# Routing two tiles further ahead, and the scatters of the gap in small lots

## The chip, the core and the metric

The kernel runs on one core of one Trainium2 chip. Its time is the device time of one execution in microseconds (us). The kernel before took 792.53 us as a median of three runs (790.85 to 795.97). A core has five engines that run their own instruction streams: TensorE (PE, whose weight loads are listed as PEld), VectorE (DVE), ScalarE (ACT), GpSimd (POOL) and SyncE (SP). They wait for one another through semaphores. POOL issues the indirect DMAs (rows sent to places that a list of numbers names), SP nearly all others.

## The reference

The input x has 4096 tokens of width 256. The reference computes, in float32:

```python
q = layernorm(x)
h = softmax((q@Wq+bq) (ctx@Wk+bk)^T per head)    # 16 heads, 77 keys
o = h @ (ctx@Wv+bv) @ Wo + bo
x = x + gamma * layernorm(q + o, eps=1e-3) + beta
f = layernorm(x)
weights, experts = top_k(softmax(f @ Wg), 4)     # 32 experts
y = sum over a token's 4 experts of weight * (silu(f@W1[e]) * (f@W3[e])) @ W2[e]
out = x + y + (silu(f@Ws1) * (f@Ws3)) @ Ws2      # the shared FFN
```

An expert takes at most 2048 (token, expert) pairs.

## The kernel before

**Stages.** Up to about 60 us the weights are prepared: Wk is folded with Wq, and Wv with Wo. Then comes the loop over 32 tiles of 128 tokens (t = 0 to 31; eight blocks of four tiles, `blk = t // 4`, `c = t % 4`), from 64 to about 394 us. Behind it stands a stretch, here called the gap, in which the shared FFN of three blocks is computed (y = block 6, block 0 and z = block 7, in this order) and the last two blocks are routed. It ends in the expert phase, which runs over tiles of 128 rows of one expert, about 1.63 us each, from about 474 to 705 us, with the shared FFN of the other blocks among them. The results are gathered and stored by 793.7.

**One tile of the loop.** `scores` makes the scores of 16 heads in three groups on PE (L430) and their maxima on DVE (L438). `soften` takes the exponentials on ACT (L446), head by head, with their sums. `invert` makes the reciprocals on DVE (L456), and `divide` multiplies on POOL (L461, three instructions of 0.97 us). One tile later `turn_p` transposes the probabilities on PE (L479), with copies on DVE (L484) and ACT (L484, L487, L488), `output` multiplies them with the folded values (L497), and `residual` adds the result and measures it (L505, L355, L356, DVE). So within tile t the order on DVE is: maxima of t, a copy for t-1, invert of t, other work, residual of t-1, and then the first maximum of t+1.

**Block work in the loop.** `scale_in`, `norm_in`, `turn_in` and `bias_in` prepare the next block's input. `keep` (L403, DVE) lays x + beta aside. `settle` (L523, L526, L355, L356, DVE) finishes the attention of one tile and measures it for the second layernorm; POOL makes the reciprocal deviations in `measure_out` and `measure_ffn`, and `norm_ffn` (ACT, with `shift`, L361, on DVE) normalises.

**Routing of a block** follows its settling, in this order: `turn_ffn` (PE transposes, ACT copies, L553, a store by SP), `gate` (L566, PE), `turn_gate` (L579, L581), `chances` (L589, L590), `powers` (ACT, L594), `choose` (top four, L603 to L612, DVE), `mark` (one-hot form of the choice, its sums and the running counts, L619, L626, L630, DVE), `count` (L638, PE), `place` (L654 to L664, DVE, three small operations on POOL). Then `send` (L674) scatters the 512 tokens' rows to the places of their experts in device memory, in 16 indirect DMAs of 128 rows: each takes POOL 0.96 us and 0.30 us of issue. `tables("a")` and `tables("z")` turn the counts into tables of the expert tiles' rows and experts; "a" covers the first 64 expert tiles, which read rows of blocks 0 to 5 only. `fetch` reads such a table into registers of SP and loads eight tiles' rows.

**What sets the order.** Nothing is planned: inside `with as_written()` every instruction of an engine is made to follow the one written before it. The one exception is a run of scatters: instructions within it have no order among themselves, so the scheduler may swap them. The routing of block `blk - 2` is written into block `blk`'s tiles: `turn_ffn` in c0; `gate`, `turn_gate`, `chances`, `powers` and `choose` in c1; `mark` in c2 ahead of `invert`; `count` and `place` in c3. Four scatters are sent per tile from t = 11. Three tiles of a block are settled one per tile behind `invert` in c0, c1 and c2, the first tile already in its own block's c3, and `keep` does two tiles in c2 and two in c3. After the loop 44 scatters are left: 12 of block 5, then 16 each of y and z. They are sent in groups of 3, 2, 7, 12 and 20.

Of the kernel before, what the change touches and what calls it, by code (L numbers as in the profile page):

```python
# [30 lines left out]
def kernel(  # L31
# [73 lines left out]
    iota_j = const.tile([P, NJ], F32, name="iota_j")  # L105
    nc.gpsimd.iota(iota_j, [[1, NJ]], base=0, channel_multiplier=0, allow_small_or_imprecise_dtypes=True)
# [260 lines left out]
    def means(name):  # L367
        return sm.tile([P, NC, 2], F32, tag="mv", name=f"mv_{name}", bufs=6)
# [300 lines left out]
    def send(blk, i0, i1):  # L669

        row, xn = rows[blk], xns[blk]
        for i in range(i0, i1):
            c = i // TOPK
            sct = nc.gpsimd.indirect_dma_start(  # L674
                out=xr,
                out_offset=bass.IndirectOffsetOnAxis(ap=row[:, i : i + 1], axis=0),
                in_=xn[:, c, :],
                in_offset=None,
            )


            tc.declare_no_dep(sct.ins, group="rows", reason="distinct rows")
            tc.add_to_no_dep_group("rows", sct.ins)
            scatters.append(sct.ins)
            if blk < BA:
                early.append(sct.ins)
            else:

                tc.declare_no_dep(sct.ins, group="firsts", reason="distinct rows")
                tc.add_to_no_dep_group("lates", sct.ins)  # L690

# [56 lines left out]
    measure_in(0)  # L748
    scale_in(0)
    norm_in(0)  # L750
    turn_in(0)
    bias_in(0)
    keep(0, 0, NC)
    xts[1] = load(1)
    with as_written():
        for t in range(NT):
            blk, c = t // NC, t % NC
            ffn, old = blk - 1, blk - 2
            ahead = blk + 1 < NB
            if c == 0 and blk + 2 < NB:  # L760
                xts[blk + 2] = load(blk + 2)
            if t == 0:

                nc.sync.dma_start(xr[NE * PLACES :, :], none)
                nc.sync.dma_start(
                    xr[: NE * PLACES, :].rearrange("(e q) r -> q e r", q=PLACES)[:P],
                    none.unsqueeze(1).to_broadcast([P, NE, ROW]),
                )
            if t == 18:
                nc.sync.dma_start(ws13[:, :, 0, :], Ws1.rearrange("(k p) f -> p k f", p=P))  # L770
                nc.sync.dma_start(ws13[:, :, 1, :], Ws3.rearrange("(k p) f -> p k f", p=P))
                nc.sync.dma_start(ws2, Ws2.rearrange("(k p) f -> p k f", p=P))
            if t in parts:
                load_experts(*parts[t])
            if c == 1 and ahead:
                scale_in(blk + 1)
            if c == 1 and ffn >= 0:
                measure_out(ffn, 2, 4)
            if c == 3 and ahead:
                bias_in(blk + 1)  # L780
            if c == 3:
                measure_out(blk, 0, 2)
            if c == 3 and ffn >= 0:
                measure_ffn(ffn)
            if c == 1 and old >= 0:
                gate(old)
            if c == 3 and old >= 0:
                count(old)
            sv = [scores(t, g) for g in range(2)]
            if c == 1 and old >= 0:  # L790
                turn_gate(old)
                chances(old)
            soften(t, 0, sv[0])
            if c == 1 and old >= 0:
                powers(old)
            soften(t, 1, sv[1])
            sv.append(scores(t, 2))
            if t >= 1:
                for i in range(3):
                    turn_p(t - 1, i)  # L800
            soften(t, 2, sv[2])
            if c == 0 and old >= 0:
                turn_ffn(old)
            if c == 2 and ahead:
                turn_in(blk + 1)
            if c == 0 and ahead:
                measure_in(blk + 1)
            if c == 1 and old >= 0:
                choose(old)
            if c == 2 and old >= 0:  # L810
                mark(old)
            if c == 3 and old >= 0:
                place(old)
            invert(t)
            divide(t)
            if c == 1 and ahead:
                norm_in(blk + 1)
            if c == 3 and ffn >= 0:
                norm_ffn(ffn)
            if c == 3:  # L820
                settle(blk, 0)
            elif ffn >= 0:
                settle(ffn, c + 1)
            if c >= 2 and ahead:
                keep(blk + 1, 2 * c - 4, 2 * c - 2)
            if t >= 11:
                b11, c11 = divmod(t - 11, NC)
                send(b11, c11 * TOPK, (c11 + 1) * TOPK)
            if t >= 1:
                residual(t - 1, output(t - 1))  # L830

        sxs[0] = late.tile([P, NC, D], F32, tag="qb", name="sx_0", bufs=3)
        sxs[0] = sxs[0].rearrange("p c d -> p (c d)").rearrange("p (k t) -> p k t", k=KC)
        nc.sync.dma_start(sxs[0], xnd[0])
        z, y = NB - 1, NB - 2
        assert BA == y
        msum_a = sm.tile([P, NE], F32, tag="msum_a", name="msum_a", bufs=1)
        nc.vector.tensor_copy(msum_a, cums[BA][:, 0, :])  # L840
        left = [(y - 1, i) for i in range(NK)]

        def sends(n):
            for blk, i in left[:n]:
                send(blk, i, i + 1)
            del left[:n]

        del left[:4]
        measure_out(z, 2, 3)
        settle(z, 1)  # L850
        sends(3)
        turn_ffn(y)
        for i in range(3):
            turn_p(NT - 1, i)
        settle(z, 2)
        residual(NT - 1, output(NT - 1))
        measure_out(z, 3, 4)
        gate(y)
        turn_gate(y)
        chances(y)  # L860
        powers(y)
        settle(z, 3)
        sends(2)
        measure_ffn(z)
    att_stack.close()

    hs_stack = ExitStack()
    hs = hs_stack.enter_context(tc.tile_pool(name="hs", bufs=1))
    tb = hs_stack.enter_context(tc.tile_pool(name="tb", bufs=1))


    tabs = {}
    e_col = tb.tile([NE, P], F32, name="e_col")
    k_a = tb.tile([NE, 1], F32, name="k_a")

    def tables(which, pairs, n):


        def small(name, dt=F32):
            return tb.tile([NE, 1], dt, tag=f"{name}_{which}", name=f"{name}_{which}")  # L880

        def wide(name, p=NE, dt=F32):
            return tb.tile([p, n], dt, tag=f"{name}_{which}" if p != NE else name, name=f"{name}_{which}")
# [12 lines left out]
        if first:  # L896
            nc.vector.tensor_scalar(e_col, ones[:NE, :], iota_p[:NE, :], None, ALU.mult)
        else:
# [20 lines left out]
        oj, t1, t2 = wide("oj"), wide("t1"), wide("t2")  # L919
        nc.vector.tensor_scalar(oj, iota_j[:NE, :n], start, None, ALU.is_ge)  # L920
        nc.vector.tensor_scalar(t1, iota_j[:NE, :n], end, None, ALU.is_ge)
# [3 lines left out]
        nc.vector.tensor_scalar(t2, iota_j[:NE, :n], base, float(P), ALU.subtract, ALU.mult)  # L925
# [5 lines left out]
        nc.vector.scalar_tensor_tensor(t2, t2, first_e, oj, ALU.add, ALU.mult)  # L931
        yield
# [3 lines left out]
        nc.tensor.matmul(p_e[:, :n], e_col, oj, start=True, stop=True)  # L936
# [11 lines left out]
        if not first:  # L948
# [3 lines left out]
            n_i = tb.tile([1, 1], I32, name="n_i")  # L952
            nc.vector.tensor_scalar(n_i, p_n[0:1, 0:1], float(RG - 1 + NA - NM_), 0.0, ALU.add, ALU.max)
            n_more = tb.tile([1, 1], I32, name="n_more")
# [3 lines left out]

    with as_written():
        for part in range(5):  # L960
            load_experts(*parts[NT + 1 + part])
        ta = tables("a", msum_a, NA)
        choose(y)
        shared_in(y, 0, AF.Tanh)
        norm_ffn(z)
        mark(y)
        sends(7)
        shared_mid(y, 0)
        next(ta)
        shared_in(y, 1, AF.Tanh)  # L970
        turn_ffn(z)
        count(y)
        gate(z)
        next(ta)
        place(y)
        assert not left
        left += [(y, i) for i in range(NK)]
        turn_gate(z)
        chances(z)
        powers(z)  # L980
        next(ta)
        shared_mid(y, 1)
        shared_in(0, 0, AF.Silu)
        choose(z)
        shared_out(y)
        next(ta)
        mark(z)
        shared_mid(0, 0)
        shared_in(0, 1, AF.Silu)
        count(z)  # L990
        msum_z = sm.tile([P, NE], F32, tag="msum_z", name="msum_z", bufs=1)
        nc.vector.tensor_copy(msum_z, cums[NB][:, 0, :])
        tz = tables("z", msum_z, NJ - NA)
        sends(12)
        place(z)
        left += [(z, i) for i in range(NK)]
        shared_mid(0, 1)
        shared_in(z, 0, AF.Silu)
# [321 lines left out]
```

## Time and profile before

| | |
|---|---|
| median of three runs | 792.53 us |
| the profiled execution | 795.5 us, of which its span 793.7 us |
| PE busy | 726.8 us, 92% of the span |
| DVE busy | 526.8 us, 66% |
| POOL busy | 403.3 us, 51% |
| ACT busy | 334.3 us, 42% |
| scatters, L674 | 128, 127.8 us busy on POOL |

Busy time is the time in which an instruction of the engine ran. In the rows that follow, a group's line, engine and operation come first, then output and input with their shapes and a count; `idle` or a bracket gives the time that the engine stood still just before, and the instruction that ended this. "remote" and "another core or an unknown queue" mean that the release could not be put down to an instruction. PEclk is the share of full clock that TensorE was granted.

### The profile page before, as it was taken

How to read it: one execution, taken by the hardware profiler on the slowest of the kernel's cores; microseconds unless marked ns; L12 is line 12 of the kernel's file. 1: busy time of each engine (PE TensorE's matmuls, PEld its weight loads, DVE VectorE, ACT ScalarE, POOL GpSimd, SP SyncE). 2: the span in 40 equal slices, each digit the busy share in tenths (PEclk: the TensorE clock that was granted, in tenths of full speed). 3: DMA queues.
4: the chain of work that ended last, by engine and by line, in shares of the span. 5: the costliest groups of instructions: out<-in, count | busy, mean ns of one | idle time of the engine just before them, and what ended most of it. 6: DMA issues, size and time to landing. Idle time of an engine off the chain costs nothing.

```text
span 793.7 us, 12911 instructions
## 1 busy us (share of the span) xinstructions
PE 726.8 (92%) x3508; PEld 540.2 (68%) x3508; DVE 526.8 (66%) x1455; ACT 334.3 (42%) x1586; POOL 403.3 (51%) x488
## 2 busy tenths in 40 slices
PE   6999999999999999999975569999999999999883
PEld 4775777677777777776743347888888878776452
DVE  1874565787778777776753336666667666564797
ACT  0647666766667776766621002222222222221100
POOL 2003333346878777786887354555555555534000
PEclk9999999999999999999999688999999999999997
DMA  8930000403226131514183523465655544522997
GB/s 270 331 107 1 1 0 2 124 10 114 79 72 213 58 130 57 155 51 142 57 243 107 159 94 110 143 209 178 210 159 170 166 158 143 175 89 74 404 396 282
DMA packets 78866, 111.96 MB, mean 141 GB/s; under 512 B 9995, under 2 KB 63679, under 8 KB 78783
## 3 DMA queue, kind: packets, MB, share of 16 engines
q1 hardware_dynamic: 59663, 66.66, 27.0%
q0 software_dynamic: 13056, 36.72, 12.8%
q10 hardware_dynamic: 6064, 7.64, 2.8%
q8 instruction: 31, 0.51, 0.3%
q14 instruction: 52, 0.43, 0.2%
HBM read 62.36 MB, written 48.64 MB: 140 GB/s over the span
## 4 chain that ended last, share of the span: by engine, by line
PE 66%; DVE 12%; ACT 6%; DMA 4%; another core or an unknown queue 4%; POOL 3%; issue 3%; SPq 0%; DVEq 0%; ACTq 0%; POOLq 0%
PE peh L1097 15%; PE po L497 14%; PE sc L430 13%; PE py L1118 7%; ACT p L446 5%; PE pgT L1089 4%; PE pp L479 2%; DVE gy L1213 2%; PE phT L1111 2%; PE ph L704 2%; DMA gy<-ys 2%; DVE y L1214 1%; POOL xr L674 1%; PE pvo L262 1%
## 5 line engine op out<-in xcount | busy, mean ns | idle before, releaser
L1123 POOL DMA_INDIRECT ys<-y,place x144 | 138.5, 962 | 120.7 <-DVE y L1122 81.0
L446 ACT ACTIVATE p<-sc,mx 128x77 f32<-128x77 f32 x512 | 159.5, 352 | 93.1 <-DVE mx L438 93.1
L1097 PE MATMUL peh<-we,gT 128*128 x576 | 151.9, 387 | 7.6 <-DVE gT L1091 7.1
L497 PE MATMUL po<-we,pT 128*128 128x256 f32 (+1 forms) x640 | 147.4, 384 | 4.6 <-DVE pT L484 3.3
L674 POOL DMA_INDIRECT xr<-xn,row x128 | 127.8, 999 | 46.5 <-issue 35.1
L461 POOL TENSOR_TENSOR p<-p,su 128x385 f32<-128x385 f32 (+1 forms) x96 | 91.1, 974 | 97.4 <-DVE su L456 76.5
L430 PE MATMUL sc<-we,qT 128*128 128x385 f32 (+1 forms) x384 | 138.9, 509 | 0.9 <-POOL qT L416 0.9
L497 PEld LDWEIGHTS po<-we,pT 128*128 128x128 f32 (+1 forms) x640 | 118.4, 190 | 27.1 <-DVE pT L484 5.4
L1105 ACT ACTIVATE h<-peh 128x128 f32<-128x128 f32 x144 | 40.0, 278 | 196.6 <-PE peh L1097 118.8
L446 ACT ACTIVATION_READ_ACCUMULATOR p<-sc,mx 128x1 f32 x512 | 119.4, 233 | 0.0
L1097 PEld LDWEIGHTS peh<-we,gT 128*128 128x128 f32 x576 | 99.9, 193 | 17.2 <-DVE gT L1091 8.4
L430 PEld LDWEIGHTS sc<-we,qT 128*128 128x128 f32 x384 | 71.1, 189 | 54.3 <-issue 27.6
L1106 DVE TENSOR_TENSOR h<-peh,h 128x128 f32<-128x128 f32 x144 | 42.0, 291 | 73.8 <-ACT h L1105 68.7
L1118 PE MATMUL py<-we,ehT 128*128 x288 | 86.6, 383 | 0.0
L1122 DVE TENSOR_SCALAR y<-py,own 128x256 f32<-128x256 f32 x144 | 69.6, 483 | 11.3 <-PE py L1118 10.3
L438 DVE TENSOR_REDUCE mx<-sc 128x5 f32<-128x385 f32 (+1 forms) x96 | 54.3, 576 | 33.2 <-PE sc L430 31.6
L1091 DVE COPY gT<-pgT 128x256 f32<-128x256 f32 x144 | 59.8, 415 | 6.7 <-PE pgT L1089 3.1
L1089 PE MATMUL pgT<-ident,g 128*128 128x128 f32 x288 | 55.6, 276 | 0.4 <-issue 0.4
L1118 PEld LDWEIGHTS py<-we,ehT 128*128 128x128 f32 x288 | 44.0, 193 | 11.9 <-issue 1.2
L1089 PEld LDWEIGHTS pgT<-ident,g 128*128 128x128 f32 x288 | 40.5, 143 | 15.1 <-issue 1.4
L730 PE MATMUL pz<-ws,hT 128*128 128x256 f32 x128 | 34.3, 419 | 15.3 <-DVE hT L719 14.4
L479 PEld LDWEIGHTS pp<-ident,p 128*128 128x128 f32 x320 | 36.1, 138 | 11.4 <-issue 5.5
(200 smaller groups left out, 933.6 us busy)
## 6 DMA issues: line engine op xcount, KB each, us to landing
g<-xr SPq DMA_DIRECT2D x144, 136.0 KB
gy<-ys SPq DMA_DIRECT2D x16, 1024.0 KB
xr<-y SPq DMA_DIRECT2D x1, 4352.0 KB
y<-in_x SPq DMA_DIRECT2D x8, 512.0 KB
out<-y ACTq DMA_DIRECT2D x16, 256.0 KB
xnd<-xnT SPq DMA_DIRECT2D x6, 512.0 KB
we<-in_W SPq DMA_DIRECT2D x8, 384.0 KB
ys<-y,place POOLq DMA_INDIRECT x144
```

The costliest lines, as they stand in the source:

```text
L430: nc.tensor.matmul(sc[:, : (h1 - h0) * SK], qTs[blk][:, k, o : o + P], mq[:, b, k, h0 * SK : h1 * SK], start=(k == 0), stop=(k == KC - 1),)
L438: nc.vector.tensor_reduce(mx[:, h0:h1], sv, AX.X, ALU.max, negate=True)
L446: nc.scalar.activation(probs[t][:, h, :], sv[:, h - h0, :], AF.Exp, bias=mx[:, h : h + 1], accum_out=su[:, h : h + 1],)
L461: nc.gpsimd.tensor_tensor(p[:, h0:h1, :], p[:, h0:h1, :], su[:, h0:h1].unsqueeze(2).to_broadcast([P, h1 - h0, SK]), ALU.mult,)
L497: nc.tensor.matmul(po[:, :D], pT[:n, i, :], vo[b][:n, i, :], start=(i == 0), stop=(i == KT - 1))
L674: sct = nc.gpsimd.indirect_dma_start(out=xr, out_offset=bass.IndirectOffsetOnAxis(ap=row[:, i : i + 1], axis=0), in_=xn[:, c, :], in_offse ...
L1089: nc.tensor.transpose(pt[:, k * P : (k + 1) * P], g[:, j % RG, k * P : (k + 1) * P], ident)
L1091: nc.vector.tensor_copy(gT.rearrange("p k t -> p (k t)"), pt[:, :D])
L1097: nc.tensor.matmul(ph[:, : 2 * H], gT[:, k, :], we[:, ds(ev[j] * EW + k * 2 * H, 2 * H)], start=(k == 0), stop=(k == KC - 1),)
L1118: nc.tensor.matmul(py[:, :D], hT, we[:, ds(ev[j] * EW + KC * 2 * H, D)], start=True, stop=True)
L1122: nc.vector.tensor_scalar(y, py[:, :D], own[:, i, 1:2], None, ALU.mult)
L1123: sent = nc.gpsimd.indirect_dma_start(out=ys, out_offset=bass.IndirectOffsetOnAxis(ap=place_[:, i : i + 1], axis=0), in_=y, in_offset=None,)
```

## The change

- In the loop, `turn_ffn` and `gate` of the block just finished (blk - 1) come in c3, between the second and third group of scores and behind `turn_p`; `turn_gate`, `chances`, `powers` and `choose` of blk - 2 in c0 of the next block, and `mark` in c0 as well, but behind `invert` and `divide`; `count` and `place` in c1. So scatters begin at t = 9, four per tile, six at t = 30 and 31.
- Tiles 1 to 3 of a block are settled all in c1, and `keep` does all four tiles in c3. The next block's input is prepared a tile or more earlier.
- In the last block everything moves up once more: block y is settled, normalised, turned, gated and chosen by t = 31, and tiles 0 and 1 of z are settled at t = 31.
- `tables("a")` runs at t = 29 to 31, in room of the one-hot form (`oh`). The column numbers `iota_j` and the constant `e_col` go; a new operation derives the numbers from another constant, and one multiplies by the expert's number.
- The first two fetches are issued right behind the loop, ahead of five loads of expert weights on SP.
- In the gap 25 scatters are sent, in lots of 3, 2, 3, 3, 3, 2, 3, 3, 3. In the lots with `last()` the first scatter written waits for the last instruction written so far. The last seven scatters are sent in the expert phase, one per seven tiles.

```diff
     def means(name):
-        return sm.tile([P, NC, 2], F32, tag="mv", name=f"mv_{name}", bufs=6)
+        return sm.tile([P, NC, 2], F32, tag="mv", name=f"mv_{name}", bufs=7)
...
+    def sends(n, after=None):
+        for i, (blk, k) in enumerate(left[:n]):
+            sct = send(blk, k, k + 1)
+            if after is not None and i == 0:
+                tc.add_manual_dep(sct, after, SYNC, reason="rows in small lots")
+        del left[:n]
+
+    def last():
+        return nc.cur_bb.bb.instructions[-1].name
...
-            if c == 3 and ffn >= 0:
-                measure_ffn(ffn)
-            if c == 1 and old >= 0:
-                gate(old)
-            if c == 3 and old >= 0:
-                count(old)
+            if c == 2 and ffn >= 0 and not end:
+                measure_ffn(ffn)
             sv = [scores(t, g) for g in range(2)]
-            if c == 1 and old >= 0:
+            if c == 1 and old >= 0:
+                count(old)
+            if c == 0 and old >= 0:
                 turn_gate(old)
                 chances(old)
+            if c == 3 and end:
+                turn_gate(y)
+                chances(y)
             soften(t, 0, sv[0])
...
             soften(t, 1, sv[1])
+            if c == 3 - end and ffn >= 0:
+                turn_ffn(ffn)
             sv.append(scores(t, 2))
             if t >= 1:
                 for i in range(3):
                     turn_p(t - 1, i)
+            if c == 3 - end and ffn >= 0:
+                gate(ffn)
+            if t >= NT - 2:
+                next(ta)
             soften(t, 2, sv[2])
-            if c == 0 and old >= 0:
-                turn_ffn(old)
...
-            if c == 1 and old >= 0:
-                choose(old)
-            if c == 2 and old >= 0:
-                mark(old)
-            if c == 3 and old >= 0:
-                place(old)
+            if c == 0 and old >= 0:
+                choose(old)
+            if c == 1 and old >= 0:
+                place(old)
+                left += [(old, i) for i in range(NK)]
...
             invert(t)
             divide(t)
+            if c == 0 and old >= 0:
+                mark(old)
+            if c == 3 and end:
+                mark(y)
...
-            if c == 3 and ffn >= 0:
-                norm_ffn(ffn)
+            if c == 1 and ffn >= 0:
+                for i in range(1, NC):
+                    settle(ffn, i)
+                if end:
+                    measure_ffn(ffn)
+            if c == 2 - end and ffn >= 0:
+                norm_ffn(ffn)
             if c == 3:
                 settle(blk, 0)
-            elif ffn >= 0:
-                settle(ffn, c + 1)
-            if c >= 2 and ahead:
-                keep(blk + 1, 2 * c - 4, 2 * c - 2)
-            if t >= 11:
-                b11, c11 = divmod(t - 11, NC)
-                send(b11, c11 * TOPK, (c11 + 1) * TOPK)
+                if end:
+                    settle(blk, 1)
+                else:
+                    keep(blk + 1, 0, NC)
+            sends(6 if t >= NT - 2 else TOPK)
             if t >= 1:
                 residual(t - 1, output(t - 1))
+            if t == NT - 3:
+                ta = tables("a", cums[BA][:, 0, :], NA)
+            if t >= NT - 3 and t < NT - 1:
+                next(ta)
...
+        measure_out(z, 2, 3)
+        count(y)
+        for i in range(3):
+            turn_p(NT - 1, i)
+        place(y)
+        left += [(y, i) for i in range(NK)]
+        settle(z, 2)
+        sends(3)
+        residual(NT - 1, output(NT - 1))
+        measure_out(z, 3, 4)
+        sends(2)
...
+        fetch(0)
+        fetch(RG)
+        for part in range(5):
+            load_experts(*parts[NT + 1 + part])
+        shared_in(y, 0, AF.Tanh)
+        settle(z, 3)
+        measure_ffn(z)
+        shared_in(y, 1, AF.Tanh)
+        shared_mid(y, 0)
+        norm_ffn(z)
+        sends(3, last())
+        shared_mid(y, 1)
+        turn_ffn(z)
+        sends(3, last())
+        shared_out(y)
+        gate(z)
+        turn_gate(z)
+        chances(z)
+        powers(z)
+        shared_in(0, 0, AF.Silu)
+        choose(z)
+        sends(3, last())
+        mark(z)
+        shared_mid(0, 0)
+        shared_in(0, 1, AF.Silu)
+        count(z)
...
+        tz = tables("z", msum_z, NJ - NA)
+        shared_mid(0, 1)
+        sends(2, last())
+        shared_in(z, 0, AF.Silu)
+        place(z)
+        left += [(z, i) for i in range(NK)]
+        shared_out(0)
+        sends(3)
+        shared_mid(z, 0)
+        shared_in(z, 1, AF.Silu)
+        shared_add(y)
+        sends(3, last())
+        shared_mid(z, 1)
+        shared_out(z)
+        shared_add(0)
+        sends(3, last())
+        shared_add(z)
...
-        fetch(0)
         for j in range(NM_ + len(steps)):
-            if j % RG == 1 and j + RG - 1 <= NM_:
+            if j % RG == 1 and RG < j + RG - 1 <= NM_:
                 fetch(j + RG - 1)
...
+            if j % 7 == 0:
+                sends(1)
```

## The prediction

> **What bounds the kernel now.** I read the page's slices first: PE is at nine or ten tenths almost everywhere, but falls to 5 to 7 in the middle, and there its clock falls too. So there are two places to cost: the loop up to there, and the gap behind it.
>
> The stretches of equal length come next (start:end, length, then busy PE, PEld, DVE, ACT, POOL, clock, DMA share, GB/s). The first two are whole blocks of the loop, the others 20 us each of the gap:
>
> ```profile
> 227.06:269.56 42.50, 42.19 (x207) 31.04 (x206) 32.69 (x91) 29.64 (x154) 32.66 (x41) 1.00 0.44 140
> 269.56:311.92 42.36, 42.03 (x206) 30.86 (x205) 32.82 (x92) 29.64 (x154) 32.75 (x41) 1.00 0.25 87
> ...
> 430.00:450.00 20.00, 4.31 (x8) 2.44 (x9) 6.30 (x17) 0.60 (x1) 8.34 (x12) 0.57 0.34 112
> 450.00:470.00 20.00, 16.42 (x59) 10.90 (x57) 5.66 (x11) 1.20 (x2) 13.93 (x15) 0.92 0.48 160
> ```
>
> A block takes 42.4 us, and PE shows 42 of them. That alone says "PE bound, DVE has 9.6 us to spare". DVE's timeline, in order of time, says more (start, duration, line, operation, idle before):
>
> ```profile
> 269.56 1.54 DVE L438 TENSOR_REDUCE mx<-sc 128x6 f32<-128x462 f32 x3
> ...
> 276.07 0.25 DVE L456 RECIPROCAL su<-su 128x16 f32<-128x16 f32 x1 [2.25 <-ACT p L446]
> ...
> 279.49 0.64 DVE L438 TENSOR_REDUCE mx<-sc 128x6 f32<-128x462 f32 x1
> ...
> 286.30 0.25 DVE L456 RECIPROCAL su<-su 128x16 f32<-128x16 f32 x1 [0.67 <-ACT p L446]
> ...
> 289.64 0.61 DVE L438 TENSOR_REDUCE mx<-sc 128x6 f32<-128x462 f32 x1
> ```
>
> The first maximum of a tile never waits for PE: it starts straight behind the residual of the tile before. From it to the reciprocal (invert) run 16 exponentials and the copies on ACT: 6.5 us (279.49 to 286.30: 6.8, with the gate's exponential in it). From there to the next first maximum DVE works without a pause. So a tile is ACT's 6.5 us plus whatever DVE is given behind invert. DVE's spare time lies ahead of invert (2.25 us before 276.07); work put there is free, work put behind it is not. By c = t mod 4 the tiles from 269.56 take 9.93, 10.15, 11.00 and 11.28, together 42.36.
>
> The gap: the chain of waits names one unknown releaser twice, for 17.95 and 15.71 us. The timeline around them:
>
> ```profile
> 439.43 0.96 POOL L674 DMA_INDIRECT xr<-xn,row  x1 [0.30 <-issue]
> ...
> 443.43 0.21 DVE L938 TENSOR_SCALAR r_tab_a<-p_r_a 1x64 int32<-1x64 f32 x1 [17.93 <-remote]
> ...
> 443.53 0.60 ACT L713 ACTIVATE sg<-ph 128x512 f32<-128x512 f32 x1 [20.81 <-remote]
> ...
> 470.60 0.96 POOL L674 DMA_INDIRECT xr<-xn,row  x1 [0.31 <-issue]
> ...
> 473.53 0.28 ACT L1105 ACTIVATE h<-peh 128x128 f32<-128x128 f32 x1 [15.73 <-remote]
> ```
>
> DVE L938 needs a product that PE ended at 425.5. Both stalls end 2 to 3 us after the last scatter of a run without rest (24 scatters to 440.4, 16 to 471.6, one per 1.27 us) and begin after some ten. Runs of 4 in the loop and 7 (410 to 419) show none. I read this as PE's release arriving only when the run ends.
>
> **The loop's change.** Duration by duration, per block:
>
> - c0 now holds choose ahead of invert (6.8) and mark behind it, which sat ahead of it in c2. Mark is L619 0.68, L626 1.06, four L630, with gaps 2.7 (293.24 to 295.92). Invert .17 and residual 1.0 (288.66 to 289.64): 6.8+.17+2.7+1.0 = 10.7.
> - c1 holds three settles in place of one: L523, L526, L355, L356 took 2.1 beside a divide (276.25 to 278.33), about 1.57 free of it. POOL's divide ends 2.9 us behind invert, so 2.1+1.9+1.6 = 5.6, and 6.5+.17+5.6+1.0 = 13.2. Place moves ahead of invert here: hidden.
> - c2 has nothing behind invert but the residual: 7.7 by DVE. The copies of p end on ACT at +5.0 (284.52), the rest of the output product takes 3.1 and the residual 1.0: 9.1.
> - c3: ACT copies xnT ahead of the last exponentials, 1.12, formerly behind them; one settle 2.1; four keeps in place of two (L403 .72 beside the divide, .48 after) 2.2: 6.5+1.1+.17+2.1+2.2+1.0 = 13.1.
>
> Together 46.1, +3.7 a block. PE does the same work and idles for it. The other moved work is hidden: shift and norm_in on ACT behind invert, measures on POOL, turn_in and count on PE, all with more than 2 us of slack; xnd's store leaves two tiles sooner on SP, whose queue has only loads due much later. Scatters from t=9 keep their four a tile (5.1 us of POOL, behind 2.9 of divide).
>
> [...] The rows (busy us, mean ns, idle before, over five and a half blocks) are
>
> ```profile
> L526 DVE SCALAR_TENSOR_TENSOR y<-qb,rs,y 128x256 f32<-128x256 f32 x24 | 24.9, 1037 | 1.6 <-DVE qb L523 0.5
> ...
> L630 DVE TENSOR_TENSOR cum<-cum,mask 128x32 f32<-128x32 f32 x22 | 4.2, 192 | 0.8
> ```
>
> but L630 ran where no divide did. L526 did run beside it and took 1.04, against 0.48 outside the loop (400.71). [...] L526 shows the contention here, so I take +4.4. Blocks 2 to 6: 22.
>
> Ends of the loop: block 0 about 0; block 1 (no old routing yet, settles and keeps as above) +2.5; block 7 +8.5 by the same sums: t=28 +1.4, t=29 +5.5 (three settles, then a shift that waits for POOL's rstd, and eleven small table operations of .14), t=30 +1.6, t=31 about 0 (second settle and mark against no keeps and less before). Loop: **+33**, 29 to 37.
>
> **The gap's change.** From the last first maximum (384.72) to the tenth expert tile's peh (491.23) is 106.5 us. I add up the changed order from invert of t=31 (+6.8), POOL by 1.27 a scatter, PE by the rows: six scatters end at +11.2; measures and place, three scatters +16.5; two +20.2; measure_ffn and norm_ffn +24.1. PE: last output +13.3, two shared_in of y +20.7, turn_ffn(z) waits to +25.0, shared_out +28.9, gate +30.3, shared_in(0) +37.5, shared_in(z,0) +41.5, shared_out(0) +45.4, shared_in(z,1) +49.0, shared_out(z) +53.9, first peh +55.2, tenth nine tiles of 1.63 and 2.8 of tables later: +72.7. With 6.8: 79.5. I add 1 for half clock after PE's idle 3 us and 2 for what is left of the stall, since the built order moves scatters without a gate ahead of gated ones (7 together, later 8): 82.5, so **-24**, -19 to -28. The nearest row to it is the two stalls, 33.6; less than that comes back because POOL's work and PE's shared FFN still stand in a row.
>
> Hidden edits: sixteen fetches go ahead of five weight loads on SP, .53 each, about 9 us; the loads land by +36 and are first needed at +55; without that cover peh waits. The new waits stand on POOL: a gated scatter waits for norm_ffn(z), the xnT copies, choose(z) or shared_mid. Behind it are queued scatters and place(z)'s three small operations alone, and nobody waits for those rows before the fetch of tile 64, in the expert loop: nil, at most 3 if place(z) comes late. Seven scatters among expert tiles: POOL is free .66 us a tile, one 1.27 per seven tiles fits; its bound is 0 to 5 if they do not. Two added table operations .25, two iotas and e_col gone: nil. The table in oh's room waits for the last mark user, nil to 1.
>
> Sum: +33 - 24 = +9. Span 793.7 + 9 = 802.7; the profiled run was 795.5, 1.8 outside its span, so 804.5; the runs' median, 792.53, lies 3.0 below that run: **801.5**.
>
> **Rivals.**
>
> *The stall returns* (the lots don't do what they say). For: 9 to 10 scatters without rest behind measure_ffn(z), 8 at the end; stalls began after about ten. Against: each such run is shorter than both that stalled. A stall of 5 to 20 in each: +10, 812 (806 to 825). Chance 0.2.
>
> *PE is the bound and DVE absorbs it* (faster). For: PE busy 42.0 of 42.4, DVE 9.6 us free per block, more than the 4.4 added; mx waits .25 to .7 for scores. If PE's queue is what paces a block, a longer c1 and c3 are made up in c2 and c0, and the loop grows by only 0 to 15, mostly in block 7. Then -24 + 9: 777 (768 to 788). It decides once the loop grows by under 24. Against: the first maximum never waits for PE. Chance 0.27.
>
> *Likeliest*, loop +33 and gap -24: 801.5, own range 791 to 811. Chance 0.53.
>
> **Numbers.** A measurement of this kernel can tell about 1% from no change: 784.6 to 800.4. The likeliest is split near that edge: 0.22 within, 0.31 slower; the stall 0.2 slower; the PE case 0.2 faster, 0.07 within. Faster 0.2, same 0.29, slower 0.51. Range 778 to 815 leaves out half of the PE case and the top of the stall case.
>
> **Signs.** Right: blocks 2 to 6 take 46 to 47 us, c1 and c3 about 13, c2 about 9; L630 or L619 lengthen behind invert; no idle of 15 us from an unknown releaser in the gap; a smaller dip of the clock; tenth peh about 82 us behind the last first maximum. Wrong: blocks near 42.4 (faster case), or a stall ending 2 to 3 us behind a run of 7 to 10 scatters. A first peh waiting for its weights would show fetch's place mattered.

## The result, and the profile after

The changed kernel takes 822.55 us (median of four runs, 820.31 to 823.16) beside 793.28 us of the kernel before (four runs): a ratio of 1.0363, with a 95% interval of 1.0323 to 1.0403. It is slower by 29 us; 801.5 was forecast. The profiled execution took 822.99 us with a span of 821.2.

The page's busy rows and clock row, after; the last row is the clock of the kernel before:

```profile
PE 740.1 (90%) x3508; PEld 546.4 (67%) x3508; DVE 521.8 (64%) x1457; ACT 333.5 (41%) x1586; POOL 402.2 (49%) x487
...
PEclk9899999999999999999987999999999999999996
PEclk9999999999999999999999688999999999999997
```

As many instructions as before do nearly as much work, in 27.5 us more. PE shows 13 us more of busy time for the same 3508 products: some ran slower. The dip of the clock in the middle is smaller, as forecast.

The span, cut at the same points in each, shows where the time went. The cuts are the first maximum of the loop, the first maximum of its last tile, and DVE's results of the tenth and the 128th expert tile; the stretch ahead (62.6 to 63.7 us) is left out. The last two rows are the same kernels profiled again in a later set of runs, and are needed below.

| us | loop | to tenth expert result | to 128th | to the end |
|---|---|---|---|---|
| before | 321.1 | 112.6 | 199.4 | 96.9 |
| after | 361.9 | 91.2 | 207.9 | 96.5 |
| before, again (e5) | 321.1 | 84.7 | 197.2 | 97.4 |
| after, again (e6) | 360.8 | 82.6 | 197.6 | 97.3 |

So the loop grew by 40.8 us, the gap shrank by 21.4, and the expert phase grew by 8.5.

Stretches of equal length, after; each is one block of the loop (start:end, length, busy PE, PEld, DVE, ACT, POOL, clock, DMA share, GB/s):

```profile
241.48:289.43 47.95, 44.21 (x206) 32.08 (x205) 32.16 (x91) 29.40 (x154) 32.75 (x41) 0.96 0.44 136
289.43:337.38 47.95, 44.22 (x206) 32.03 (x205) 32.16 (x91) 29.40 (x154) 32.72 (x41) 0.96 0.18 66
```

A block takes 47.95 us where it took 42.4. DVE has 16 us free in it, and PE nearly 4: neither engine is full, so neither one's total sets the length. The clock is 0.96 where it was 1.00. DVE's timeline of the c0 and c1 tiles of one block says what paces it:

```profile
289.43 1.07 DVE L436 TENSOR_REDUCE mx<-sc 128x6 f32<-128x462 f32 x2
...
296.14 0.25 DVE L454 RECIPROCAL su<-su 128x16 f32<-128x16 f32 x1 [1.48 <-ACT p L444]
296.31 0.63 DVE L617 TENSOR_TENSOR oh<-iota_e,idx 128x512 f32<-128x512 f32 x1
296.97 1.05 DVE L624 TENSOR_REDUCE mask<-oh 128x128 f32<-128x512 f32 x1
298.05 1.78 DVE L628 TENSOR_TENSOR cum<-cum,mask 128x32 f32<-128x32 f32 x4
...
300.83 1.55 DVE L436 TENSOR_REDUCE mx<-sc 128x6 f32<-128x462 f32 x3
...
307.70 0.25 DVE L454 RECIPROCAL su<-su 128x16 f32<-128x16 f32 x1 [3.11 <-ACT p L444]
...
314.53 1.54 DVE L436 TENSOR_REDUCE mx<-sc 128x6 f32<-128x462 f32 x3
```

It is the pattern of the kernel before: 6.7 to 6.9 us of ACT from first maximum to invert, then DVE's own work without a pause. Mark now stands in that second part, and its four L628 took 1.78 us beside POOL's divide, where the kernel before had 0.87 (295.05) with no divide running. In c1 DVE idles 3.1 us ahead of invert and then does 6.8 us of settling and residual. The four tiles take 11.40, 13.70, 10.11 and 12.74 us, where 10.7 (11.4 with the 0.7 by which the +4.4 lies above the sum of +3.7), 13.2, 9.1 and 13.1 were forecast.

In the gap no wait of 15 us is left. But the waits by engine and line (us in total, times, longest) show shorter ones of the same kind:

```profile
DVE rmx L587 <- remote: 10.8, 1, 10.8
...
ACT pr L577 <- remote: 7.8, 1, 7.8
```

ACT's L577 waits for gate(z), whose last product PE ended at 463.21, and ran at 467.62, just as a run of nine scatters without rest, from 456.2, ended at 467.5. So the lots of three did not stay small, as the rival *The stall returns* had said. The same happens in the expert phase. POOL's timeline there, and then ACT's:

```profile
546.94 0.96 POOL L1144 DMA_INDIRECT ys<-y,place  x1 [1.26 <-DVE y L1143]
548.21 0.96 POOL L672 DMA_INDIRECT xr<-xn,row  x1 [0.30 <-issue]
549.48 0.96 POOL L1144 DMA_INDIRECT ys<-y,place  x1 [0.30 <-issue]
550.74 0.96 POOL L1144 DMA_INDIRECT ys<-y,place  x1 [0.30 <-issue]
552.01 0.96 POOL L1144 DMA_INDIRECT ys<-y,place  x1 [0.30 <-issue]
```

```profile
554.12 0.28 ACT L1126 ACTIVATE h<-peh 128x128 f32<-128x128 f32 x1 [3.73 <-remote]
```

One of the seven scatters (L672) makes POOL late; it catches up with the expert results (L1144) at 1.27 us each, without rest, and ACT and DVE get PE's releases only 1.1 us after the last of them. PE then waits for DVE. Of the seven scatters five come behind the tenth result (522.0, 535.2, 548.2, 561.5 and 575.0). Each is followed, 4 to 7 us later, by one step of 3.2 to 3.7 us from result to result where 1.63 is usual; when the same kernel ran without stalls (e6) no such step is there. The 8.5 us are 1.7 for each.

The trace also records when the semaphores rose. In the kernel before, PE's four products of the long wait ended at 425.31, 425.67, 427.58 and 429.30; PE's semaphore, which DVE and ACT wait for, stood still in the records from 422.10 to 443.40 and then rose four times within 0.2 us. In e5, without stalls, it rose 0.01 to 0.02 us behind the same four ends. So in this execution it was the release that came late, not the product, and not DVE's start.

### The profile page after: what moved, and what is told of

The parts are those of the page before. It is cut to its first block, busy times and chain, and to the rows that moved or that the text cites. A ratio compares the mean times of both kernels' runs of the same rounds, so it can differ in the third digit from the quotient of the medians.

```text
span 821.2 us, 12909 instructions
## 1 busy us (share of the span) xinstructions
PE 740.1 (90%) x3508; PEld 546.4 (67%) x3508; DVE 521.8 (64%) x1457; ACT 333.5 (41%) x1586; POOL 402.2 (49%) x487
## 4 chain that ended last, share of the span: by engine, by line
PE 53%; DVE 17%; ACT 14%; DMA 7%; issue 5%; POOL 3%; another core or an unknown queue 0%; SPq 0%; DVEq 0%; ACTq 0%; POOLq 0%
PE peh L1118 14%; ACT p L444 10%; PE po L495 10%; PE py L1139 7%; PE sc L428 6%; PE pgT L1110 4%; PE ph L703 3%; DVE y L524 2%; DVE mx L436 2%; DVE st L353 2%; PE phT L1132 2%; DMA gy<-ys 2%; DMA out<-y 2%; PE pvo L260 2%; PE pz L729 1%
## 5 line engine op out<-in xcount | busy, mean ns | idle before, releaser
L1144 POOL DMA_INDIRECT ys<-y,place x144 | 138.5, 962 | 118.6 <-DVE y L1143 71.5
L495 PE MATMUL po<-we,pT 128*128 128x256 f32 (+1 forms) x640 | 158.6, 404 | 20.4 <-DVE mx L436 13.6
L495 PEld LDWEIGHTS po<-we,pT 128*128 128x128 f32 (+1 forms) x640 | 125.4, 201 | 47.1 <-issue 20.3
L1118 PE MATMUL peh<-we,gT 128*128 x576 | 149.4, 382 | 8.0 <-DVE gT L1112 5.9
L672 POOL DMA_INDIRECT xr<-xn,row x128 | 128.2, 1001 | 46.2 <-issue 35.1
L459 POOL TENSOR_TENSOR p<-p,su 128x385 f32<-128x385 f32 (+1 forms) x96 | 89.1, 954 | 123.0 <-DVE su L454 76.3
L428 PE MATMUL sc<-we,qT 128*128 128x385 f32 (+1 forms) x384 | 141.7, 511 | 0.9 <-POOL qT L414 0.9
L436 DVE TENSOR_REDUCE mx<-sc 128x5 f32<-128x385 f32 (+1 forms) x96 | 52.3, 574 | 30.2 <-PE sc L428 21.6
L454 DVE RECIPROCAL su<-su 128x16 f32<-128x16 f32 x32 | 8.1, 253 | 77.5 <-ACT p L444 77.5
```

The costliest lines, as they stand in the source:

```text
L428: nc.tensor.matmul(sc[:, : (h1 - h0) * SK], qTs[blk][:, k, o : o + P], mq[:, b, k, h0 * SK : h1 * SK], start=(k == 0), stop=(k == KC - 1),)
L436: nc.vector.tensor_reduce(mx[:, h0:h1], sv, AX.X, ALU.max, negate=True)
L459: nc.gpsimd.tensor_tensor(p[:, h0:h1, :], p[:, h0:h1, :], su[:, h0:h1].unsqueeze(2).to_broadcast([P, h1 - h0, SK]), ALU.mult,)
L495: nc.tensor.matmul(po[:, :D], pT[:n, i, :], vo[b][:n, i, :], start=(i == 0), stop=(i == KT - 1))
L672: sct = nc.gpsimd.indirect_dma_start(out=xr, out_offset=bass.IndirectOffsetOnAxis(ap=row[:, i : i + 1], axis=0), in_=xn[:, c, :], in_offse ...
L1118: nc.tensor.matmul(ph[:, : 2 * H], gT[:, k, :], we[:, ds(ev[j] * EW + k * 2 * H, 2 * H)], start=(k == 0), stop=(k == KC - 1),)
```

## The experiments

Two things were open: why the loop cost more than the sum said, and what the long waits of the gap are. The experiments ran on five chips, each beside the kernel before. On four of them the kernel before took 764 to 771 us, on one (e13, e14) 795, where the first measurement had 793. What that is became a question of its own. Where no interval is given, an experiment's time is that of a single execution.

**Mark ahead of invert (e1).**

```diff
             if c == 0 and old >= 0:
                 choose(old)
+                mark(old)
...
             divide(t)
-            if c == 0 and old >= 0:
-                mark(old)
```

> The changed kernel, with mark in c0 put back ahead of invert. Theory (a tile is ACT's 6.5 us plus what DVE has behind invert): the four L628 fall from 1.78 to 0.87 us since no divide runs beside them; choose and mark fill DVE to about +8.0, where invert then comes; behind it only the residual, so c0 falls from 11.4 to the 10.1 that c2 shows as PE's floor, -1.3 in each of six blocks, about -8 in all (815). Rival (PE's queue paces a block, DVE absorbs): c0 stays at 11.4 or its gain comes back in c1, and the time is within 2 us of 822.5.

Measured: 785.43 us beside 769.77 of the kernel before; the changed kernel itself, where the kernel before takes 768, takes 803.5 (e6). So 18 us, not 8, though on another chip. DVE's timeline of that c0 tile:

```profile
279.65 1.07 DVE L436 TENSOR_REDUCE mx<-sc 128x6 f32<-128x462 f32 x2
...
286.71 0.87 DVE L628 TENSOR_TENSOR cum<-cum,mask 128x32 f32<-128x32 f32 x4
287.50 0.24 DVE L454 RECIPROCAL su<-su 128x16 f32<-128x16 f32 x1
...
289.00 0.64 DVE L436 TENSOR_REDUCE mx<-sc 128x6 f32<-128x462 f32 x1 [0.24 <-PE sc L428]
```

Invert comes 7.85 us behind the first maximum, with no idle ahead of it, and c0 takes 9.36. L628 is back at 0.87: beside the divide it had taken 0.9 more (1.78). The floor of 10.1 that I had read from c2 was none: c0 fell below it, c1 from 13.70 to 13.38, and c2 from about 10.0 to 9.16, the 9.1 of the prediction. What c2's extra us was shows in PE's timeline. First the changed kernel (e6), with the stretches of its output product; then e1:

```profile
311.26 1.25 PE L477 MATMUL pp<-ident,p 128*128 128x128 f32 x10
315.23 6.08 PE L495 MATMUL po<-we,pT 128*128 128x256 f32 x20 [2.71 <-DVE pT L482]
```

```profile
302.80:307.20 4.40, 4.40 (x23) 3.88 (x22) 1.25 (x5) 4.24 (x22) 2.00 (x7) 1.00 0.11 35
315.20:317.20 2.00, 1.97 (x5) 1.63 (x6) 1.86 (x8) 2.00 (x15) 1.33 (x3) 0.50 0.21 70
317.20:319.20 2.00, 2.00 (x8) 1.63 (x7) 0.01 (x1) 2.00 (x13) 0.00 (x0) 0.72 0.00 0
```

```profile
304.67 1.97 PE L495 MATMUL po<-we,pT 128*128 128x256 f32 x8 [1.15 <-DVE pT L482]
307.10 2.86 PE L495 MATMUL po<-we,pT 128*128 128x256 f32 x12 [0.47 <-ACT pT L482]
```

With c0 and c1 longer, PE runs out of work before c2 and stands still for 2.71 us; it comes back at half clock (0.50, then 0.72), and twenty matmuls take 6.08 us. In the tile before, at full clock, they took 4.5. With 1.15 us of idle, in e1, the clock stayed whole (1.00 from 304.6 to 306.6). So DVE's late work can be paid for twice: in its own tile, and as PE's clock in the next.

The same pause does not always cost the clock. In the third block of e3, with the changed kernel's loop, it left the clock whole:

```profile
173.27 1.96 PE L495 MATMUL po<-we,pT 128*128 128x256 f32 x8 [2.71 <-DVE pT L482]
175.70 2.86 PE L495 MATMUL po<-we,pT 128*128 128x256 f32 x12 [0.47 <-ACT pT L482]
```

That tile took 9.16 us, the 9.1 of the prediction. Blocks 2 to 6 of the five traces with this pause (the first measurement, e6, e2, e3, e10) hold it 25 times: in 20 half clock followed and c2 took 9.85 to 10.27, in five (two of e3, two of e10, one of e2) none did and c2 took 9.16. So c2's extra 0.7 to 1.1 us is the half clock. In the first measurement it was granted 0.50 for 3.41 us in each of the five blocks (317.32 to 320.73 in the block shown above). Why the five pauses of e2, e3 and e10 left the clock whole was not shown.

**Keeps two and two (e2), turn_ffn behind the exponentials (e10).**

```diff
-                else:
-                    keep(blk + 1, 0, NC)
+            if c >= 2 and ahead:
+                keep(blk + 1, 2 * c - 4, 2 * c - 2)
```

> The changed kernel, with the four keeps of c3 split again, two in c2 and two in c3. Theory: in c2 DVE stands 1.8 us waiting for the output product, so two keeps (1.3 us) are free there, and c3 loses 1.0: 12.74 to 11.7 with c2 still at 10.1; seven blocks, about -7 (815.5). Rival (PE's queue paces a block): the block stays at 47.95.

```diff
+            if c == 0 and old >= 0:
+                gate(old)
             sv = [scores(t, g) for g in range(2)]
...
-            if c == 3 - end and ffn >= 0:
+            if c == 3 - end and ffn >= 0 and end:
                 turn_ffn(ffn)
...
-            if c == 3 - end and ffn >= 0:
+            if c == 3 - end and ffn >= 0 and end:
                 gate(ffn)
...
             soften(t, 2, sv[2])
+            if c == 3 and ffn >= 0 and not end:
+                turn_ffn(ffn)
```

> The changed kernel with turn_ffn behind the last exponentials of c3 again and gate at the head of the next tile (blocks 0 to 5). Theory: the two copies of xnT (1.12 us) leave the stretch between first maximum and invert, which falls from 7.51 to 6.5 in c3, and c3 from 12.74 to 11.7; about -6 over six blocks (797, if the kernel before takes 768). Rival: PE's transposes then hold up c0's scores, and c0 takes the gain back.

Measured: e2 798.8 us. c3 fell by 0.68 to 12.06 (two keeps there are 0.68 shorter, not 1.0), and c2 stayed between 9.2 and 10.3. e10 took 796.78: invert in c3 came at 6.54 instead of 7.51, and c3 fell by 0.97 to 11.77, with c0 unchanged at 11.40. Each alone behaves as an addition to a chain does, and neither is absorbed.

**Two put back (e7), three put back (e11).** e7 has the edits of e1 and e2, e11 those of e10 as well.

> The changed kernel with mark in c0 ahead of invert and the keeps two and two in c2 and c3. The two alone took 3.3 and 0.7 us off a block. If they add, a block takes 44.0 (9.36 + 13.4 + 9.2 + 12.06) and the loop up to the last first maximum 404 us; the time is 20 to 24 us below the changed kernel's beside it. If PE's queue takes some back, c2 grows to 10 and the block stays at 44.7.

> The changed kernel with all three put back: mark ahead of invert, keeps two and two, turn_ffn behind the exponentials. Left of the loop's edits are the three settles in c1. Theory: c0 9.8, c1 13.5, c2 9.2, c3 11.1, together 43.6 against 42.36, so the settles' own price is about 1.2 a block; time 777 to 780 where the kernel before takes 768. Rival: a block cannot fall below 44 since PE waits elsewhere.

Measured: e7 783.91 us, ratio to the kernel before 1.0211 (1.0164 to 1.0258); a block takes 44.56 (9.79, 13.55, 9.16, 12.06). e11 780.65, a block 44.0 (10.09, 13.56, 9.16, 11.20). Of the 5.6 us that a block grew in the first measurement, 4.0 are thus the places of mark, keeps and turn_ffn, the clock's part among them; 1.6 stay with the three settles in c1 and whatever else of the loop's change e11 keeps. No run moves the settles alone.

Together the three do not add. c3 loses its 0.68 in e7 as in e2, but the block falls only from the 44.65 of e1 to 44.56, not to 44.0: c0 and c1 grow by 0.43 and 0.17. In c0 DVE now waits for PE's scores, where e1 had no wait (e7's timeline):

```profile
234.33 0.56 DVE L436 TENSOR_REDUCE mx<-sc 128x5 f32<-128x385 f32 x1 [0.40 <-PE sc L428]
...
235.73 0.56 DVE L436 TENSOR_REDUCE mx<-sc 128x5 f32<-128x385 f32 x1 [0.25 <-PE sc L428]
```

e11's block stops at the 44.0 that its rival named. PE is idle for 1.9 us of it, 1.8 of them in c2; in the other three tiles it has no more than 0.2. So near 44 us PE is full outside c2, and the 1.6 us of growth that are left are about as long as its pause there.

**The seven scatters in the gap (e3).** They are sent behind the last lots, with a short power on POOL between.

```diff
         sends(3, last())
...
+        nc.gpsimd.tensor_tensor(rest, rest, neg_half, ALU.pow)
+        sends(4)
+        nc.gpsimd.tensor_tensor(rest, rest, neg_half, ALU.pow)
         shared_add(z)
+        sends(3)
...
-            if j % 7 == 0:
-                sends(1)
```

> The changed kernel, with the seven last scatters sent at the end of the gap (a short power on POOL, about 1 us, ahead of and between lots of 4 and 3) and none in the expert phase. Theory (each extra scatter makes POOL catch up with a run of five or more without rest, in which PE's releases are held for 2 to 3 us): from tile 9's result to tile 127's takes 199.5 us as in the kernel before, not 207.9, and the gap gets 2 to 8 longer; in all 814 to 822. Rival (the expert phase is slower for the earlier fetches or the order of weight loads): it stays at 207 to 208.

Measured: 802.1 us; from the tenth result to the 128th 197.5 us. That looks like the theory, but the changed kernel has 197.6 with its seven scatters where the kernel before takes 768 (e6). There they cost nothing, so the agreement is chance and this run can't tell.

**The same two kernels again (e5, e6).**

> The kernel before, unchanged, profiled again: beside the four experiments so far it took 769.8 us, not 793. Theory A (the two stalls of the gap are not in every execution; where they are missing the gap is that much shorter): at 770 its trace shows no wait of 15 us from an unknown releaser and the first expert tile's result at 65 to 75 us behind the last first maximum; at 793 it shows both and +93.6. Theory B (the whole chip ran faster): at 770 the loop's blocks are shorter than 42.36 as well.

> The changed kernel, unchanged, timed beside the kernel before. Theory A: where the kernel before takes 770, the change has only its dearer loop to show, +40 on the loop and at most a few us won back in the gap, so 800 to 810, ratio 1.04 to 1.05; where it takes 793, 820 to 823 and 1.036. If instead the gap's 21 us are won from the order of the work, the ratio is 1.036 or less in both.

Measured: e5 764.91 us, e6 803.5 beside 767.91, ratio 1.0478 (1.043 to 1.0527). The loop of e5 is the same to a tenth (321.1); what is missing is the stalls. DVE's wait for the table product:

```profile
423.15 0.21 DVE L938 TENSOR_SCALAR r_tab_a<-p_r_a 1x64 int32<-1x64 f32 x1 [1.32 <-PE p_r_a L934]
```

It is 1.3 us where it was 17.93, in the middle of the same run of scatters without rest, which goes on to 459.9. The first expert result comes at 63.6 instead of 93.6, and the clock row shows no dip. So a run without rest is not enough: the wait in it was 17.93 us in the first measurement and 1.32 in e5. Theory A holds. Where there are no stalls, the changed gap wins only 2.1 us, and the change loses more.

**Rests among the scatters (e4; again as e8, e12, e13).** The kernel before, with a power on POOL (1.04 us) behind every fourth scatter of the gap's longer lots.

```diff
...
-            for blk, i in left[:n]:
+            for k, (blk, i) in enumerate(left[:n]):
                 send(blk, i, i + 1)
+                if k % 4 == 3:
+                    nc.gpsimd.tensor_tensor(rest, rest, neg_half, ALU.pow)
```

> The kernel before, with a power of about 1 us on POOL behind every fourth scatter of the gap's lots of 7, 12 and 20; nothing else. Theory (a run of scatters without rest holds back PE's releases until it ends): no wait of 15 us from an unknown releaser is left, the first expert tile's result comes 75 to 85 us behind the last first maximum instead of 93.6, and the time falls by 8 to 18 (775 to 785). Rival (it is the number of scatters in flight, rests or none): the two stalls stay and POOL's nine rests add up to 9 us (793 to 802).

> The kernel before with the nine rests. It tells something new only if the kernel before beside it takes about 793, with the long stalls: then 772 to 782 if rests let PE's releases through, 793 or more if they do not. Beside 768 it takes 775 to 778 as before.

Measured, three times without stalls: 777.44 (beside 769.77), 776.73 (ratio 1.0127, 1.008 to 1.0175) and 777.69. The first lies in the range of e4's theory by chance: there was no stall to take away, and the rests cost 8 us. The rests push the last scatters back, and the results of expert tiles 5 to 7 wait for POOL: the tenth result comes at 95.5 to 95.9 instead of 84.7. The fourth time, e13, the kernel before beside it took 795.38, with stalls, and the rests 780.31. The same wait there (L942 in that kernel):

```profile
424.45 0.21 DVE L942 TENSOR_SCALAR r_tab_a<-p_r_a 1x64 int32<-1x64 f32 x1 [1.30 <-issue]
```

In this run the first expert result came at 64.8, the tenth at 98.5. With 1.04 us of other work on POOL behind every fourth scatter the long stall was gone (1.30 us), with the same 44 scatters behind the loop: the long stalls went with the run without rest, and not with the number of scatters. That rests on one execution with rests beside two without (795.38, and e14 with its stall), all on one chip. Some 3 us are left, shorter holds by my estimate: without stalls the same kernel took 776.7 to 777.7.

The traces tell the two conditions apart in one more way. Those of the first measurement and of e13 and e14 hold 7327 to 7493 rises of semaphores, the other fourteen 11897 to 11965: where releases came late, over a third of the records was missing. e13 is among the four, so it ran in the condition with stalls and had no long one. Whether the loss of records and the late releases have one cause, and whether the recording itself has a part in it, was not tested; executions of which no profile is kept took as long (790.85 to 795.97).

**Ten scatters in the expert phase (e9, e14).** The kernel before, with one part of the change: block 7's last ten scatters are sent one per five expert tiles.

```diff
-        sends(20)
-        assert not left
+        sends(10)
...
+            if j % 5 == 0:
+                sends(1)
```

> The kernel before with one part of the change alone: the last ten of block 7's scatters are sent in the expert phase, one per five tiles; its loop and the rest of its gap stay. Theory: without the long stalls the first expert results come 63.6 us behind the last first maximum, but POOL has scatters until 76 and the results of tiles 5 to 7 wait for it (from 72.0 to 80.3 where 3.3 is usual). With ten fewer this wait goes: -4 to -5 us against the kernel before beside it, and the expert phase does not grow, since POOL has 0.36 us to spare a tile. Rival (each scatter there costs its 1.2 us, as in the first trace of the changed kernel): +7 or more.

> The kernel before with ten scatters in the expert phase. Beside a kernel before of 793: the second stall (15.7 us, behind 16 scatters) shrinks by the length of ten, 12.7 us, but each of the ten costs about 1.2 in the expert phase, as in the first trace of the changed kernel: 790 to 795. Beside 768: 761 to 763.

Measured: e9, without stalls, 761.72 us beside 767.99, ratio 0.9923 (0.99 to 0.9946). It is the fastest kernel of the study. The tenth result comes at 81.4 instead of 84.7, and the expert phase stays at 197.3. e14, on the chip of e13 beside 795.38, took 803.07, 8 us above what was expected. Its first stall is there:

```profile
425.62 18.04 another core or an unknown queue
```

This is a line of its chain of waits. The second stall is shorter: the first result comes at 84.1 and the tenth at 106.7, 6 us earlier than in the first measurement. But from tenth to 128th it takes 210.1 us, 10.7 more than the 199.4 of the kernel before with stalls: seven of the ten scatters come there, 1.5 us each, near the 1.7 of the changed kernel. One part of the change, then, wins 6 us where there are no stalls and, by one execution each, loses 8 where there are.

**Rests of eight (e15; again as e16).** As e4, but behind every eighth scatter: three rests.

> The kernel before with a rest behind every eighth scatter of the gap's lots (three rests, about 1 us each) in place of nine. Beside a kernel before of 793 to 795: if runs of eight let PE's releases through, 770 to 778, below the 780.3 of nine rests; if they are too long, stalls of 8 us and more come back and it takes 785 to 795. Beside 768: three rests put the last scatters back by about 4 us and the time by 2 to 4, 770 to 772.

Measured: 771.88 us, ratio 1.0061 (1.0041 to 1.0081), and 770.05; both ran without stalls, so whether runs of eight are short enough where stalls occur was not seen. The changed kernel's own trace answers in part: there PE's releases came about 4 us late behind a run of nine in the gap, and 2 to 3 behind runs of five in the expert phase.

## Why the prediction was wrong

Two steps failed: the loop's idle time of PE was put at nothing, and the scatters of the expert phase were counted as fitting into POOL's free time. A third, the gap, came out near its number for another reason than the one given.

*What paces a block* was right for the changed kernel. The block follows ACT's stretch and then DVE's work behind invert; each edit that moved work between the two parts, taken alone, moved its tile by about its size. The rival in which PE paces and DVE absorbs is out there: with 16 us of DVE and nearly 4 of PE free, blocks took 48. It is not out below: near 44 us (e7, e11) DVE waits for PE's scores and gains are absorbed. "The first maximum never waits for PE" had left out that PE was all but full at 42.4.

*The loop's size* was too small: +40.8 for +33. Per term: c0 11.40, for which 10.7 had been summed and 0.7 added (in the +4.4) for mark beside the divide. No run shows that 0.7; what the runs showed in its place is 0.9 for the four L628 (1.78 beside the divide, 0.87 without). L617, which began 0.2 us ahead of the divide, took 0.63 (0.68 ahead of invert in the kernel before); there the divide's first instruction took 1.21 us, where it took 0.96 in c2 with DVE idle. c1 13.70 for 13.2, as invert came at 6.9 and not 6.5. c3 12.74 for 13.1. c2 10.11 for 9.1, the largest: "PE does the same work and idles for it" had PE's idle time in it, but no price for it, and in 20 of 25 pauses it cost PE half its clock for 3.41 us. Where the clock stayed whole, c2 took 9.16. A block took +5.6 where +4.4 was taken, which is 5.9 us over five blocks; block 7 took +9.7 for +8.5; block 1 +2.5, as said; block 0 +0.7 for 0.

*The gap's -24* came out at -21.4, but it was not what I took it for. The table takes it apart: 27.9 us are stalls of the kernel before that only some sets of runs have (112.6 against 84.7), 2.1 are won by the order of the work (84.7 against 82.6), and 8.6 are lost again to the changed kernel's own stalls (91.2 against 82.6). That this comes near 24 is in part luck. I had read a stall seen in one execution as a property of the kernel.

*"POOL is free .66 us a tile"* is the step that failed outright. A scatter takes 0.96 and 0.30 of issue, so of 1.63 us a tile 0.36 is free. The slip alone would have cost nothing: seven tiles of 0.36 still hold one scatter of 1.27, and in e6 the phase is no longer than without (197.6 and 197.2). What was left out is that an extra scatter makes POOL run without rest for about four tiles. I had read the stalls as PE's releases held by such runs; I used that reading for the gap and not for the expert phase. It cost 8.5 us where the bound was 0 to 5.

*The stall returns* was given 0.2 as a rival, with 5 to 20 us. It did return: runs of nine in the gap, since the scheduler moves scatters without a gate ahead as the built order showed, and runs of five in the expert phase. The sign named for it, a stall that ends behind a run of 7 to 10 scatters, came. "Each such run is shorter than both that stalled" was no reason against it. The first expert result came at 73.2 in the first measurement and at 64.5 without stalls: 8.7 us.

The misses add up: 7.8 on the loop, 2.6 on the gap, 8.5 in the expert phase and -0.4 at the end, 18.5 us together: the span was to be 802.7 and was 821.2. The rest of the 21 us is the 3.0 by which the median was taken to lie below the profiled run; after, it lay 0.4 below. Without stalls the changed kernel took 803.5, near the 801.5 that was forecast, but that is chance: the kernel before took 768 there, and the change cost 36 us in place of 9.

## What to carry to other kernels

When two engines take turns on a chain, the free time of each lies at one place of the cycle. Work belongs into the stretch where its engine waits for the other, and moving it to the far side of that wait costs its whole length, however idle the engine looks over the block. A wait whose releaser had long been done should be profiled again, on another chip, before a change is built on it. An engine's slack has to be counted with its issue time (0.30 us behind each 0.96 here), and idle time of an engine with its price, where its clock was seen to fall behind it (0.50 for 3.41 us behind 2.71 us of idle here).

## What the runs showed of the hardware

- In the first measurement and on one of five later chips PE's releases reached ACT and DVE only 0.1 to 3 us behind the end of a run of POOL's indirect DMAs issued one behind the other (0.96 us and 0.30 us of issue): 17.9 us late behind 23 (in lots of 7, 12 and 4, with about 0.5 us of small operations between), about 4 us behind nine, 2 to 3 behind five. On the other four chips the kernel before took 767 to 770 us (medians) in place of 793 and 795, and in its trace there (e5) the same wait was 1.3 us in the same order of instructions. With a POOL operation of 1.04 us behind every fourth the long wait was gone (1.30 us; 780.31 beside 795.38). In the traces with late releases over a third of the semaphore records is missing (7327 to 7493 beside 11897 to 11965). Why sets of runs differ stays open: each was on one chip, so chip and moment can't be told apart.
- After a pause of 2.71 us TensorE was granted half clock for 3.41 us in 20 of 25 cases (0.50 from 317.32 to 320.73 in the first measurement), and stayed at full clock in five. After the pause of 1.15 us in e1 it stayed at 1.00. What told the five from the 20 was not shown.
- The four additions L628 took 1.78 us beside POOL's divide, 0.87 without it (the kernel before at 295.05, e1 at 286.71). Where L617 had begun 0.2 us ahead of the divide, it took 0.63 us and the divide's first instruction 1.21, in place of 0.96 in c2.
